# Two state-space layers and two attention layers on one core: the order of scan phases over images, the round of a projection, and the admission limit on TensorE

## The chip, the cores and the metric

The kernel runs on one core of one Trainium2 chip. The metric is device time in microseconds (us) of one execution, lower is better; the time of a version is the median of its runs. The engines are named as in the profile: PE (TensorE matmul; PEld is its weight load), DVE (VectorE), ACT (ScalarE), POOL (GpSimd), SP (SyncE, which issues the DMAs here).

## The reference

The input is four images of 56 x 56 positions with 96 channels (L = 3136 positions). Four layers follow one another.

- Layer 0: layer norm, a projection to u and z (192 channels each), a selective scan of u in four directions (rows forward and back, columns forward and back), a weighted sum of the four, times silu(z), an output projection with shortcut, then a feed-forward block with gelu.
- Layer 1: the same kind of scan with other weights, with a 3 x 3 depthwise convolution and silu ahead of it, a norm and a product with silu(z) behind it, and beside it a branch of depthwise 3 x 3 convolution, relu and pointwise convolution; the two are fused, normed and added to the input.
- Layers 2 and 3: attention without softmax, and a feed-forward block in a small float format.

The scan is what costs most. For each direction, channel d (192) and state n (16), along the 3136 positions:

```
dt = softplus(W_dt @ (W_x @ u)[:rank] + bias)          # per channel and position
h[d, n] = exp(dt[d] * a[d, n]) * h[d, n] + dt[d] * u[d] * B[n]
y[d]    = sum over n of C[n] * h[d, n]   (+ D[d] * u[d])
```

The images are independent of one another; layer 1 of an image needs layer 0 of the same image only.

## The kernel before

**Phases, chunks, rounds.** A phase is the scan of one layer of one image. There are eight, all of layer 0 first (images 0 to 3), then all of layer 1. A phase has four directions (`ORDER`, pairs of orientation and reversal; orientation 1 reads the columns, so that PE, ACT and POOL read and write the tiles with a stride of 56 elements, called vertical below), a direction has seven chunks of 448 positions, and a chunk has eight rounds r = 4e + q: e is the half of the channels (96 each), q a quarter of the states. That makes 8 x 4 x 7 x 8 = 1792 rounds. In a round, 128 partitions hold 4 states x 32 channels, and three groups g hold the 96 channels.

**One round** (function `scans`, L660 to L700). PE spreads B over the partitions by a bf16 matmul into `b` (`spread_b`, L574). DVE multiplies v = du x b (L667), for two or three of the groups; where it does two, POOL makes the third ahead of time (L645). Which rounds DVE does alone is given by `OWN = (3, 4, 6)`, and by `OWN_TAIL = (3, 4)` in layer 1 from image 1 on. ACT makes the decays da = exp(dt x a) in PSUM (L637), DVE runs three scans of 448 steps (L689), POOL multiplies by C into `hc` (L699), and two rounds later PE adds up over the states into `y` (`add_up`, four matmuls at L727). When a new sum starts, at q = 0, so in rounds r = 2 and 6, PE first loads `y` with the sum of the directions so far, or with D x u (L723, fp32, strided if vertical). ACT copies `y` out (L734). Scan state is carried from chunk to chunk by small ACT copies (L693, L652).

**Preparing the next chunks.** While a chunk is scanned, the next one is prepared (`prepare`, `prepare_on_scalar`): its rows are copied out of PSUM in r = 0 (`rows`, L467 and L469), the step sizes are made by matmuls in r = 1 and 3 (`step_size`, L480) with exp and ln on ACT in r = 2 and 3 (L489, L490), multiplied by u on POOL (L496), parked in DRAM and fetched back spread over the partitions. The chunk after that is begun (`prepare_ahead`): its projection `W_x @ u`, two fp32 matmuls (`project_step`, L428), goes out in r = 6 and r = 7. L428 and L480 share one PSUM buffer, `pp`. The first chunk of an image loads U in r = 5.

**Zero matmuls.** `keep_busy` (L706) adds matmuls with zero weights to the open sum (L714): per round `WARM` = 7.3 less the work counted since the last round, where `spend` (L922) counts work at 1.6 per unit of PE. `add_up` adds two more at q = 0.

**Work beside the scans.** Everything else runs in pieces between the half rounds. `beside` lists what starts with which phase: `load` of images 1 to 3 with phase 0, `middle(i)` (end of layer 0, start of layer 1 of image i) with phases 1 to 4, `fuse(i)` (end of layer 1) and `attend(i)` (layers 2 and 3) with phases 5 to 7; what is left runs alone after the last scan (`late`). A part is a generator that stops at each yield with a place (half round C or F, PSUM banks held) and a cost on ACT (a) and PE (p). `overlap` (L892) lets it go on when `room` (L930) finds the backlog plus its cost within `ACT_LIMIT` = 4.0 and `PE_LIMIT` = 5.0; each half round takes `SPARE` = (0.9, 2.4) off the backlog. The scans count their own PE work by constants of 1.3 (L670). Inside the scans the order of instructions on PE, ACT, DVE and POOL is the order in which this program issues them, and each engine works through its list in order.

**Diagonals.** The depthwise convolutions are matmuls with diagonal weights (L876), which POOL builds (`diagonals`, L858): 18 for `middle` once, and 9 for `fuse` once, in the same buffer.

Of the kernel before, what the change touches and what calls it, by code (L numbers as in the profile page):

```python
# [19 lines left out]
NB = 4  # L20
# [5 lines left out]
NE = 2  # L26
NG = 3
NQ = 4
# [3 lines left out]
NCW = L // CW  # L32
# [6 lines left out]
OWN = (3, 4, 6)  # L39
OWN_TAIL = (3, 4)  # L40

SPARE = (0.9, 2.4)
ACT_LIMIT, PE_LIMIT = 4.0, 5.0
BANKS, LATE_BANKS = 2, 4
DEPTH, LATE_DEPTH = 3, 6

# [4 lines left out]
WD = NE * 128 + NE * C + NE + NE * NQ * NG  # L51

EXP_AND_LN = 6

# [108 lines left out]
class Net:  # L165
    def __init__(self, ctx, tc, aps, at, out):
        self.tc, self.nc, self.aps, self.at, self.out = tc, tc.nc, aps, at, out
        pool = lambda name, **kw: ctx.enter_context(tc.tile_pool(name=name, **kw))
        self.const = pool("const", bufs=1)
        self.big = pool("big", bufs=1)  # L170
        self.psum = pool("psum", bufs=1, space=bass.MemoryType.PSUM)
        self.dram = pool("dram", bufs=1, space=bass.MemoryType.DRAM)
        self.nw, self.nwin, self.depth, self.banks, self.ring = NW, NWIN, DEPTH, BANKS, None
        self.setup()
        self.dg = None
        self.kept = (0, 0, 0)
        self.ready = set()
        self.live, self.g = [], {}
        self.backlog, self.paced = [0.0, 0.0], False
        self.work, self.tables = 0.0, False  # L180
        self.U = [self.big.tile([C, L], F32, name=f"U{e}") for e in range(NE)]
        self.Y = [self.big.tile([C, L], F32, name=f"Y{e}") for e in range(NE)]
        self.wp = pool("work", bufs=2)
        self.scan_pool = ExitStack()
        self.sp = self.scan_pool.enter_context(tc.tile_pool(name="scan", bufs=2))
        self.pool = pool
        d = lambda name, *shape: [self.dram.tile(list(shape), F32, name=f"{name}{i}") for i in range(NB)]
        self.xd, self.xrd = d("x", C, L), d("xr", C, L)
        self.ud, self.zd, self.yd, self.md = d("u", DI, L), d("z", DI, L), d("y", DI, L), d("m", DI, L)
# [17 lines left out]
    def par(self, group, name):  # L207
        a, n = self.at[group][name]
        return self.tiles[group][:, a : a + n]
# [350 lines left out]

    def prepare_ahead(self, far, r):

        if far is not None:
            if r == 2:
                self.parameters(far)
            elif r == 5:
                self.inputs(far)
            elif r > 5:
                self.project_step(far, r - 6)

    def spread_b(self, ch, q):

# [16 lines left out]
    def scans(self):  # L589
# [6 lines left out]

        nc, sp = self.nc, self.sp
        chunks = []
        for l in range(2):
            for i in range(NB):  # L600
                for n, (orient, rev) in enumerate(ORDER[l]):
                    for step in range(NCS):
                        ch = Step()
                        ch.l, ch.i, ch.orient, ch.rev, ch.step = l, i, orient, rev, step
                        ch.k = 2 * orient + rev if l == 0 else orient + 2 * rev
                        ch.c = NCS - 1 - step if rev else step
                        ch.n, ch.first = n, n == 0 and step == 0
                        ch.skip = n == 0
                        ch.last = n == 3 and step == NCS - 1
                        for n_ in ("dt", "du", "cb", "dtc", "duc", "dtd", "dud"):  # L610
                            setattr(ch, n_, [])
                        chunks.append(ch)
        first, second = chunks[:2]
        self.parameters(first)
        self.inputs(first)
# [23 lines left out]
        def begin(n):  # L639
            ch, e, q = rounds[n]  # L640
            b = self.spread_b(ch, q)
            v = sp.tile([128, NG, CS + 2], F32, name="v", bufs=3)
            ahead = NQ * e + q not in (OWN_TAIL if ch.l and ch.i else OWN)
            if ahead:
                nc.gpsimd.tensor_tensor(v[:, 2, TOKENS], ch.du[e][:, 2], ch.cb[q][:, 1], ALU.mult)  # L645
            return b, v, ahead
# [13 lines left out]
        for n, (ch, e, q) in enumerate(rounds):  # L660
            r = NQ * e + q
            c = 1 if ch.step else 0
            way = slice(CS + c, 0, -1) if ch.rev else slice(1 - c, CS + 1)
            end = 1 if ch.rev else CS
            b, v, ahead = nxt
            for g in range(2 if ahead else 3):
                nc.vector.tensor_tensor(v[:, g, TOKENS], ch.du[e][:, g], b, ALU.mult)  # L667
            self.prepare(ch, nexts.get(ch), r)
            self.half_round()
            self.spend((0.7, 0, 1.3, 1.3, 0, 0, 0, 0)[r], (0, 1.3, 0, 1.3, 0, 0, 1.3, 1.3)[r] + 1.3 * (r % NQ == 2))  # L670
            yield "F", n, r
            self.prepare_on_scalar(nexts.get(ch), r)
            ended = late.pop(0) if len(late) == 2 else None
            if ended:
                self.keep_busy(ended[2])
            more = n + 1 < len(rounds)
            if more:
                nxt = begin(n + 1)
            if ended:
                self.add_up(*ended)  # L680
            self.prepare_ahead(afters.get(ch), r)
            self.half_round()
            for g in range(NG):
                if g == 1:
                    yield "C", n, r
                if g == 2 and ended and ended[2] == NQ - 1:
                    self.spend(0.6, 0)
                    self.keep_sums(*ended[:3])
                nc.vector.tensor_tensor_scan(  # L689
                    v[:, g, way], da[g][:, way], v[:, g, way], 0.0, ALU.mult, ALU.add  # L690
                )
                if g == 2 and ch.step < NCS - 1:
                    nc.scalar.copy(ch.par.carry[:, e, q].unsqueeze(2), v[:, :, end : end + 1])  # L693
                if more:
                    decay(n + 1, g)
                    if g == 0:
                        carried(n + 1, nxt[1])
            hc = sp.tile([128, NG, CS], F32, name="hc", bufs=3)
            nc.gpsimd.tensor_tensor(hc, v[:, :, TOKENS], ch.cb[q][:, 0].unsqueeze(1).to_broadcast([128, NG, CS]), ALU.mult)  # L699
            late.append((ch, e, q, hc))  # L700
# [30 lines left out]
    def keep_sums(self, ch, e, q):  # L731

        y = self.in_order(self.Y[e], ch.orient, ch.c * CS, CS)
        self.nc.scalar.copy(y, self.y[:C].rearrange("p (a b) -> p a b", b=HS))  # L734
        if ch.n < 3:
            return
        s = slice(ch.c * CS, (ch.c + 1) * CS) if ch.orient == 0 else slice(0, L)
        if ch.orient == 0 or ch.last:
            self.nc.sync.dma_start(self.yd[ch.i][C * e : C * e + C, s], self.Y[e][:, s])
        if e == NE - 1:  # L740
            self.kept = (ch.l, ch.i, ch.step + 1)

# [105 lines left out]
    def diagonals(self, *weights):  # L850

        t = self.wp.tile([128, 9, 192], F32, name="dg", bufs=1)
        out, n = [], 0
        for w in weights:
            p = w.shape[0]
            d = t[:p, :, n : n + p]
            for tap in range(9):
                self.nc.gpsimd.tensor_scalar_mul(d[:, tap], self.ident[:p, :p], w[:, tap : tap + 1])  # L858
                yield "F0"
            out.append(d)  # L860
            n += p
        return out

    def conv(self, diag, win, lo, *parts):

# [94 lines left out]
    def middle(self, i):  # L960
# [45 lines left out]

        yield from self.overlap(part, NCW)

        if self.dg is None:
            self.dg = yield from self.run(self.diagonals(par("c128", "1conv_wa"), par("c128", "1conv_wb")[:64]))  # L1010
        dga, dgb = self.dg

        def convolve(c):
# [24 lines left out]
            nc.sync.dma_start(self.ud[i][128:, s], t)  # L1038

        yield from self.overlap(convolve, NCW, 2)  # L1040
        self.ready.add((1, i))

    def run(self, part):
# [11 lines left out]
    def fuse(self, i):  # L1055

        nc = self.nc
        par = self.par
        if len(self.dg) > 1:
            self.dg = yield from self.run(self.diagonals(par("c96", "1dw_w")))  # L1060
        (dgx,) = self.dg

        def part(c):
# [61 lines left out]
            yield from self.gram(0, i, c, x, s)  # L1125


        yield from self.overlap(part, NCW, ready=lambda c: self.kept >= (1, i, c + 1))

    def attend(self, i):  # L1130

# [141 lines left out]
def tile_net(ctx: ExitStack, tc: tile.TileContext, aps, at, out):  # L1273
# [5 lines left out]
    def alone(lanes):  # L1279
# [4 lines left out]

    alone([net.load(0)])

    beside = [
        [net.load(1), net.load(2), net.load(3)], [net.middle(0)], [net.middle(1)], [net.middle(2)], [net.middle(3)],
        [net.fuse(0), net.attend(0)], [net.fuse(1), net.attend(1)], [net.fuse(2), net.attend(2)],
    ]  # L1290
    rounds = 4 * NCS * NE * NQ
    E = mybir.EngineType
    with tc.manual_schedule(engines={E.PE, E.Activation, E.DVE, E.Pool}):
        net.exp_and_ln()
        lanes = []
        for slot, n, r in net.scans():
            p, u = divmod(n, rounds)
            net.slot, net.paced = slot, True
            if slot == "C" and u == 2 and p < 8:

                assert p > 5 or not lanes
                lanes.append(chain(*beside[p]))
                if p == 7:
                    lanes.insert(0, chain(net.fuse(3), net.attend(3)))
            if n > 1 and p < 8:
# [23 lines left out]
```

## Time and profile before

| | before |
|---|---|
| median of 3 runs | 8809.27 us (8805.61 to 8817.11) |
| the profiled execution's own time | 8833.83 us |
| its span in the profile | 8832.1 us |
| first scan starts, last scan ends | 118 us, 8462 us |
| phases 0 to 3 (layer 0) | 1040, 1033, 1028, 1027 us |
| phases 4 to 7 (layer 1) | 1043, 1067, 1055, 1050 us |
| after the last scan | 370 us |
| zero matmuls (L714) | 6066, busy 1631.0 us |
| mean granted PE clock | 0.90 |

In the profile, a group has the line, the engine, the operation, how many, and its busy time. A matmul with fp32 operands makes two rows. A row of the busy time by stretch has the stretch (us from the span's start), its length, then busy us and instructions of PE, PEld, DVE, ACT and POOL, the granted PE clock, the DMA share and GB/s. A row of the waits has who waited for whom, the total in us, how often, and the longest. Ends of matmuls are modelled, so PE shows as busy somewhat beyond its work.

### The profile page before, as it was taken

The page shows a single profiled execution, that of the slowest core. Times are in us where ns is not written, and L with a number is a line of the kernel's source. Part 1 is how long each engine was busy: PE and PEld are TensorE (multiplying, and loading weights), DVE is VectorE, ACT ScalarE, POOL GpSimd, SP SyncE. Part 2 cuts the span into 40 slices and gives each one's busy share as a digit, 9 for nine tenths or more (in the row PEclk, how much of TensorE's full clock was granted, in tenths as well). Part 3 has the DMA queues.
Part 4 walks back from the last instruction along what each step waited for, and adds up shares of the span by engine and source line. Part 5 has one row for each costly group of instructions (what it writes and reads, how often), then busy time and mean ns, then how long its engine had stood idle before and what let it go on. Part 6 is the DMA issues. An engine that isn't in the chain of part 4 may idle for free.

```text
span 8832.1 us, 122725 instructions
## 1 busy us (share of the span) xinstructions
PE 7589.0 (86%) x34408; PEld 2805.6 (32%) x34408; DVE 7950.4 (90%) x10933; ACT 5910.0 (67%) x12541; POOL 7597.3 (86%) x4075
## 2 busy tenths in 40 slices
PE   6888888797889888898889978988899888998897
PEld 3332223232333223332233323333233332333344
DVE  5999999989998999989998999999999999999941
ACT  5777667676776667766676655667666677666636
POOL 4888999989998999989988899899999999989930
PEclk8888989899998999989898889988899888998986
DMA  5677677677777677766776676667776667666721
GB/s 145 165 175 170 159 186 174 157 167 170 181 163 168 152 182 173 173 160 149 188 171 164 155 175 164 147 152 166 181 168 158 145 162 188 165 157 155 172 73 46
DMA packets 951348, 1418.02 MB, mean 161 GB/s; under 512 B 176578, under 2 KB 943812, under 8 KB 949796
## 3 DMA queue, kind: packets, MB, share of 16 engines
q1 hardware_dynamic: 949888, 1408.37, 67.1%
q8 instruction: 270, 4.42, 0.2%
q14 instruction: 418, 3.42, 0.1%
q10 hardware_dynamic: 772, 1.80, 0.1%
HBM read 1141.42 MB, written 268.14 MB: 160 GB/s over the span
## 4 chain that ended last, share of the span: by engine, by line
PE 43%; DVE 28%; ACT 10%; issue 9%; DMA 5%; POOL 2%; SPq 1%; DVEq 0%; POOLq 0%; ACTq 0%
DVE v L689 20%; PE y L727 8%; DVE v L667 7%; PE y L714 6%; PE y L723 6%; PE pp L428 5%; PE ps L876 4%; ACT da L637 3%; PE b L574 3%; PE pp L480 3%; DMA du<-dd 2%; POOL hc L699 1%; PE ps L779 1%; PE ps L799 1%; DMA cb<-cd 1%
## 5 line engine op out<-in xcount | busy, mean ns | idle before, releaser
L699 POOL TENSOR_TENSOR hc<-v,cb 128x1344 f32<-128x1344 f32 x1792 | 5169.4, 2885 | 662.6 <-DVE v L689 377.6
L689 DVE TENSOR_TENSOR_SCAN v<-da,v 128x449 f32<-128x449 f32 (+1 forms) x5376 | 5521.6, 1072 | 57.9 <-ACT v L652 33.1
L637 ACT ACTIVATE da<-dt,na 128x448 f32<-128x448 f32 x5376 | 3396.5, 634 | 1475.5 <-DVE v L689 1445.0
L667 DVE TENSOR_TENSOR v<-du,b 128x448 f32<-128x448 f32 x4172 | 2332.5, 605 | 247.1 <-PE b L574 181.1
L727 PE MATMUL y<-hc,four 128*32 128x448 f32 x14336 | 1937.3, 616 | 1.8 <-POOL hc L699 1.7
L714 PE MATMUL y<-w,zeros 128*96 128x448 bf16 x6066 | 1631.0, 389 | 0.0
L574 PE MATMUL b<-cf,sel 128*128 128x448 bf16 x1792 | 675.5, 377 | 1025.6 <-DVE v L667 1021.1
L645 POOL TENSOR_TENSOR v<-du,cb 128x448 f32<-128x448 f32 x1204 | 1373.5, 1141 | 97.1 <-DMA cb<-cd 58.2
L714 PEld LDWEIGHTS <-zeros 128*96 128x96 bf16 x6066 | 738.4, 130 | 1364.2 <-issue 1143.6
L428 PE MATMUL pp<-U,wd 96*128 96x448 f32 x896 | 691.6, 860 | 12.3 <-DMA U<-u 12.3
L727 PEld LDWEIGHTS y<-hc,four 128*32 128x32 f32 x14336 | 295.6, 113 | 1157.4 <-issue 727.2
L723 PE MATMUL y<-Y,ident 96*96 96x448 f32 x672 | 546.3, 903 | 37.6 <-ACT Y L734 23.0
L496 POOL TENSOR_TENSOR duc<-dtc,U 96x448 f32<-96x448 f32 x448 | 560.4, 1251 | 4.6 <-ACT dtc L490 4.6
L876 PE MATMUL ps<-win,dg 64*64 64x220 f32 (+9 forms) x1980 | 528.7, 467 | 5.9 <-ACT w L1023 5.0
L693 ACT COPY carry<-v 128x3 f32<-128x3 f32 x1536 | 298.4, 194 | 278.2 <-DVE v L689 277.3
L480 PE MATMUL pp<-cf,wd 12*96 12x448 f32 (+1 forms) x896 | 469.4, 605 | 0.9 <-ACT cf L469 0.8
L489 ACT ACTIVATE dtc<-pp,wd 96x448 f32<-96x448 f32 x448 | 279.2, 623 | 254.3 <-PE pp L480 252.8
L587 POOL TENSOR_TENSOR cf<-cf 64x448 f32<-64x448 f32 x448 | 417.3, 931 | 35.8 <-ACT cf L467 0.8
L734 ACT COPY Y<-y 96x448 f32<-96x448 f32 x448 | 339.3, 757 | 42.6 <-PE y L727 41.6
L876 PEld LDWEIGHTS ps<-win,dg 64*64 64x64 f32 (+2 forms) x1980 | 233.9, 162 | 353.7 <-issue 301.6
L723 PEld LDWEIGHTS y<-Y,ident 96*96 96x96 f32 x672 | 118.6, 187 | 640.9 <-ACT da L637 290.2
L428 PEld LDWEIGHTS pp<-U,wd 96*128 96x128 f32 x896 | 156.8, 219 | 450.1 <-issue 384.8
(423 smaller groups left out, 6050.0 us busy)
## 6 DMA issues: line engine op xcount, KB each, us to landing
cb<-cd SPq DMA_DIRECT2D x3584, 112.0 KB, 4.3
dt<-dd SPq DMA_DIRECT2D x1792, 168.0 KB, 4.4
du<-dd SPq DMA_DIRECT2D x1792, 168.0 KB, 4.2
dd<-dtc SPq DMA_DIRECT2D x448, 168.0 KB, 2.0
dd<-duc SPq DMA_DIRECT2D x448, 168.0 KB, 2.1
U<-u SPq DMA_DIRECT2D x112, 168.0 KB, 4.6
z<-w SPq DMA_DIRECT2D x56, 224.0 KB, 3.0
u<-w SPq DMA_DIRECT2D x56, 224.0 KB, 3.5
```

The costliest lines, as they stand in the source:

```text
L428: self.nc.tensor.matmul(ch.ps.rearrange("p (a b) -> p a b", b=HS), ch.par.wx[:, e], self.in_order(self.U[e], ch.orient, ch.c * CS, CS), st ...
L480: self.nc.tensor.matmul(ps[:C], ch.par.wt[rows, C * e : C * e + C], ch.cf[rows], start=True, stop=True)
L574: self.nc.tensor.matmul(ps, self.sel[:, q], self.upper(ch.cf), start=True, stop=True)
L637: nc.scalar.activation(da[g][:, TOKENS], ch.dt[e][:, g], AF.Exp, scale=ch.par.na[:, e, q, g : g + 1])
L645: nc.gpsimd.tensor_tensor(v[:, 2, TOKENS], ch.du[e][:, 2], ch.cb[q][:, 1], ALU.mult)
L667: nc.vector.tensor_tensor(v[:, g, TOKENS], ch.du[e][:, g], b, ALU.mult)
L689: nc.vector.tensor_tensor_scan(v[:, g, way], da[g][:, way], v[:, g, way], 0.0, ALU.mult, ALU.add)
L699: nc.gpsimd.tensor_tensor(hc, v[:, :, TOKENS], ch.cb[q][:, 0].unsqueeze(1).to_broadcast([128, NG, CS]), ALU.mult)
L714: self.nc.tensor.matmul(self.y[:C], self.zeros, self.some, start=False, stop=False)
L723: nc.tensor.matmul(o, w, self.in_order(a, ch.orient, ch.c * CS, CS), start=True, stop=False)
L727: nc.tensor.matmul(self.y[32 * n : 32 * n + 32], self.four, hc[:, g], start=n == 3, stop=n == 3 or q == NQ - 1,)
L876: self.nc.tensor.matmul(o[:, a - r0 : e - r0, x0:x1], diag[:, tap], win[:, a + dy - lo : e + dy - lo, x0 + dx : x1 + dx], start=n == 0, st ...
```

## The change

1. **Order of phases.** `PHASES = ((0,0), (0,1), (1,0), (0,2), (1,1), (0,3), (1,2), (1,3))`, pairs of layer and image. With phase p starts the work that the phase before it has made possible: `middle(i)` after layer 0 of image i, `fuse(i)` and `attend(i)` after layer 1. So fuse and attend run from phase 3 on; two such parts can be open at a time, and `middle` is put in front.
2. **Projection.** `project_step` goes out in r = 4 and 5, except for the first chunk of an image (r = 6 and 7).
3. **Accounting.** The scans count L723 and the projection's matmuls at 1.5, or 3.0 if vertical, and in the round in which they go out. `PE_LIMIT` is 7.0.
4. **OWN_TAIL** holds from phase 3 on (`LATE_ROUND`), instead of phases 5 to 7.
5. **Diagonals.** They are rebuilt whenever `middle` and `fuse` take turns, and a part waits until nobody uses the other kind.

```diff
+PHASES = ((0, 0), (0, 1), (1, 0), (0, 2), (1, 1), (0, 3), (1, 2), (1, 3))
+
-ACT_LIMIT, PE_LIMIT = 4.0, 5.0
+ACT_LIMIT, PE_LIMIT = 4.0, 7.0
...
+LATE_ROUND = 3 * 4 * NCS * NE * NQ
...
     def prepare_ahead(self, far, r):
-        if far is not None:
-            if r == 2:
-                self.parameters(far)
-            elif r == 5:
-                self.inputs(far)
-            elif r > 5:
-                self.project_step(far, r - 6)
+        if far is None:
+            return
+        if r == 2:
+            self.parameters(far)
+        elif r == 5:
+            self.inputs(far)
+        e = self.projected(far, r)
+        if e in (0, 1):
+            self.project_step(far, e)
+
+    def projected(self, far, r):
+        return r - (6 if far.first else 4)
...
-        for l in range(2):
-            for i in range(NB):
+        for l, i in PHASES:
...
-            ahead = NQ * e + q not in (OWN_TAIL if ch.l and ch.i else OWN)
+            ahead = NQ * e + q not in (OWN_TAIL if n >= LATE_ROUND else OWN)
...
-            self.spend((0.7, 0, 1.3, 1.3, 0, 0, 0, 0)[r], (0, 1.3, 0, 1.3, 0, 0, 1.3, 1.3)[r] + 1.3 * (r % NQ == 2))
+            far = afters.get(ch)
+            strided = [1.5 + 1.5 * ch.orient] * (r % NQ == 2)
+            if far and self.projected(far, r) in (0, 1):
+                strided.append(1.5 + 1.5 * far.orient)
+            self.spend((0.7, 0, 1.3, 1.3, 0, 0, 0, 0)[r], 1.3 * (r in (1, 3)) + sum(strided))
...
+    def diagonal(self, kind, *weights):
+
+        while self.dg_users and self.dg_kind != kind or self.dg_kind == "":
+            yield
+        if self.dg_kind != kind:
+            self.dg_kind = ""
+            self.dg = yield from self.run(self.diagonals(*weights))
+            self.dg_kind = kind
+        self.dg_users += 1
...
-        if self.dg is None:
-            self.dg = yield from self.run(self.diagonals(par("c128", "1conv_wa"), par("c128", "1conv_wb")[:64]))
+        yield from self.diagonal("conv", par("c128", "1conv_wa"), par("c128", "1conv_wb")[:64])
...
-        yield from self.overlap(part, NCW, ready=lambda c: self.kept >= (1, i, c + 1))
+        yield from self.overlap(part, NCW, ready=lambda c: self.kept.get((1, i), 0) > c)
+        self.dg_users -= 1
...
+    beside = [[net.load(1), net.load(2), net.load(3)]]
+    beside += [[net.fuse(i), net.attend(i)] if l else [net.middle(i)] for l, i in PHASES[:-1]]
...
-                assert p > 5 or not lanes
-                lanes.append(chain(*beside[p]))
+                lanes.insert(len(lanes) * PHASES[p - 1][0], chain(*beside[p]))
```

More of the change, by code (lines that the diff above doesn't have):

```diff
@@ L175, in __init__ @@
         self.dg = None
-        self.kept = (0, 0, 0)
+        self.kept = {}
+        self.dg_kind, self.dg_users = None, 0
         self.ready = set()
@@ L598, in scans @@
         chunks = []
-        for l in range(2):
-            for i in range(NB):
[L601 to L612, printed above, removed]
+        for l, i in PHASES:
+            for n, (orient, rev) in enumerate(ORDER[l]):
+                for step in range(NCS):
+                    ch = Step()
+                    ch.l, ch.i, ch.orient, ch.rev, ch.step = l, i, orient, rev, step
+                    ch.k = 2 * orient + rev if l == 0 else orient + 2 * rev
+                    ch.c = NCS - 1 - step if rev else step
+                    ch.n, ch.first = n, n == 0 and step == 0
+                    ch.skip = n == 0
+                    ch.last = n == 3 and step == NCS - 1
+                    for n_ in ("dt", "du", "cb", "dtc", "duc", "dtd", "dud"):
+                        setattr(ch, n_, [])
+                    chunks.append(ch)
         first, second = chunks[:2]
@@ L740, in keep_sums @@
         if e == NE - 1:
-            self.kept = (ch.l, ch.i, ch.step + 1)
+            self.kept[ch.l, ch.i] = ch.step + 1
     def factor(self, *x):
@@ L1058, in fuse @@
         par = self.par
-        if len(self.dg) > 1:
-            self.dg = yield from self.run(self.diagonals(par("c96", "1dw_w")))
+        yield from self.diagonal("dw", par("c96", "1dw_w"))
         (dgx,) = self.dg
@@ L1125, in part @@
             yield from self.gram(0, i, c, x, s)
-        yield from self.overlap(part, NCW, ready=lambda c: self.kept >= (1, i, c + 1))
+        yield from self.overlap(part, NCW, ready=lambda c: self.kept.get((1, i), 0) > c)
+        self.dg_users -= 1
     def attend(self, i):
@@ L1285, in tile_net @@
     alone([net.load(0)])
[L1287 to L1290, printed above, removed]
+    beside = [[net.load(1), net.load(2), net.load(3)]]
+    beside += [[net.fuse(i), net.attend(i)] if l else [net.middle(i)] for l, i in PHASES[:-1]]
     rounds = 4 * NCS * NE * NQ
```

## The prediction

> **What bounds the kernel now.** I read the page first.
>
> ```profile
> span 8832.1 us, 122725 instructions
> PE 7589.0 (86%) x34408; PEld 2805.6 (32%) x34408; DVE 7950.4 (90%) x10933; ACT 5910.0 (67%) x12541; POOL 7597.3 (86%) x4075
> PE 43%; DVE 28%; ACT 10%; issue 9%; DMA 5%; POOL 2%; SPq 1%; DVEq 0%; POOLq 0%; ACTq 0%
> DVE v L689 20%; PE y L727 8%; DVE v L667 7%; PE y L714 6%; PE y L723 6%; PE pp L428 5%; PE ps L876 4%; ACT da L637 3%; PE b L574 3%; PE pp L480 3%; DMA du<-dd 2%; POOL hc L699 1%; PE ps L779 1%; PE ps L799 1%; DMA cb<-cd 1%
> ```
>
> DVE is the fullest engine, yet PE carries more of the chain, so the two take turns. The busy time by stretch, cut at the first scan of each phase, shows how much is left to win. Lines 1 and 3 are phases 3 (layer 0, image 3) and 5 (layer 1, image 1), line 2 is the tail after the last scan.
>
> ```profile
> 3219.39:4246.58 1027.19, 877.24 (x3980) 305.81 (x3980) 970.55 (x1275) 705.56 (x1442) 933.00 (x491) 0.92 0.72 169
> 8461.71:8832.10 370.39, 313.45 (x1386) 187.07 (x1384) 77.60 (x243) 192.88 (x443) 31.09 (x28) 0.76 0.17 47
> 5289.56:6356.26 1066.70, 937.22 (x4315) 345.83 (x4314) 998.08 (x1401) 694.00 (x1565) 969.02 (x531) 0.90 0.69 161
> ```
>
> Over the eight phases the scans take 8343 us and DVE is busy for 7852, so 491 us of DVE idle and 370 us of tail are all there is. DVE's waits inside the scans name the idle time's causes:
>
> ```profile
> DVE v L667 <- PE b L574: 181.1, 179, 3.9
> DVE ps L794 <- ACT rs L792: 80.9, 54, 5.5
> DVE v L689 <- ACT v L652: 33.1, 49, 2.1
> ```
>
> The rest is small: some 75 us in waits on PE by the phase work, 50 on POOL and "issue". To see where b is late I cut one chunk of phase 3 that carries a convolution (37.5 us) into its rounds r=0 to 7:
>
> ```profile
> 3890.72:3895.82 5.10, 5.10 (x28) 1.71 (x28) 4.12 (x7) 3.44 (x7) 3.49 (x3) 1.00 1.08 225
> 3895.82:3900.34 4.52, 4.52 (x18) 1.55 (x18) 4.12 (x7) 3.92 (x8) 4.36 (x4) 1.00 0.84 196
> ...
> 3913.62:3918.17 4.55, 2.85 (x23) 1.10 (x22) 4.55 (x8) 4.51 (x7) 3.94 (x2) 1.00 0.93 227
> 3918.17:3922.18 4.01, 3.58 (x9) 0.77 (x12) 4.01 (x7) 3.29 (x8) 3.44 (x3) 0.73 1.09 236
> 3922.18:3928.24 6.06, 6.06 (x34) 1.86 (x27) 4.11 (x6) 2.12 (x5) 6.03 (x4) 0.90 1.08 269
> ```
>
> In r=5 PE has 2.85 us to do and DVE is full; in r=7 and r=0 PE is solid and DVE loses 2 and 1 us. A chunk without phase work (4036.75 to 4071.18) takes 34.4 us with 33.9 of DVE: nothing to win there. Averaged over layer 1, vertical chunks, the time from scan to scan is 5.75 us after r=7 and 5.32 after r=0, 4.3 to 5.1 elsewhere.
>
> **Projection moved (r=6, 7 to r=4, 5).** The chain through that chunk gives PE's price of each step: two vertical L428 rows 1.82 us, L723 1.65, four L727 0.89, L480 0.92, one L714 0.20, b 0.2 to 0.3, six convolution rows 2.4. In horizontal chunks the timeline has the next start 0.75 us after L723's. L428 stands in r=6 beside L723 today and r=4, 5 have little. I added these prices up along the instruction order of both kernels, from one b matmul to the next. Vertical layer 1 chunks go from 3.1, 2.6, 6.5, 5.0 (r=4 to 7) to 4.0, 4.3, 5.5, 3.5. PE can run about 3 us (one round's scans) ahead of DVE, so what hurts is pairs of rounds: their sum over 10.5 us (two DVE rounds of 4.25 plus 2) totals 215 us before, 102 after. The 181 us of waits for b should fall in that proportion at best; since a convolution chunk's five heaviest rounds (r=4 to r=0) stay near 26 us (25.7 before, 26.6 after), I keep 55%: **-80 us**. The phase work's own waits (about 155 us) queue behind the same PE work: -30 (0 to -60). The moved step waits on more: `pp` has one buffer, and the L489 read of the second step size in r=3 must finish before L428 starts in r=4. ACT does that in r=3's second half (623 ns), and what would queue behind a late L428 is b of the round after; half of that in each of 224 chunks, 70 us, bounds it; PE's spare time in r=3 hides it, I take 0. The first chunk of an image keeps r=6, and SP's queue is untouched: 9450 SP instructions in both orders.
>
> **Zero matmuls.** Because the strided matmuls are now counted at 1.5 or 3.0, 951 of 6066 L714 go: 951 x 0.20 = 190 us of PE. L714 is 6.6% of the chain inside the scans, 550 us for 6066, so at most 86 us of path; that is part of the pair sums above and is not counted again. Against it stands the clock. Consecutive 3.41 us stretches of the quiet chunk:
>
> ```profile
> 4056.53:4059.94 3.41, 1.75 (x12) 0.41 (x11) 3.41 (x5) 1.75 (x5) 3.41 (x3) 1.00 0.92 217
> 4059.94:4063.35 3.41, 0.52 (x2) 0.32 (x2) 3.41 (x6) 2.14 (x5) 3.39 (x2) 1.00 1.02 239
> 4063.35:4066.76 3.41, 3.41 (x12) 0.56 (x10) 3.41 (x6) 2.12 (x5) 2.84 (x3) 0.50 1.03 229
> ```
>
> A stretch with 0.52 us of PE is followed by one at half clock; one with 1.75 isn't. Over all such stretches of the trace (each matmul's end taken 0.16 us earlier, for the pipeline) every one under 35% busy was followed by half clock, about two thirds at 35 to 45%, and 4 of 1263 above 75%. The Trainium skill, "TensorE: Matmul & The Clock Gate", section "Why this matters for your kernels", asks only for no idle gap over about 3 us. By that rule the removed zeros are free, since no round loses all its work, and the whole 86 us could come (8563 on top of my sum); by the rows the limit lies near 40% busy, and thinner rounds can halve the clock. In the after order r=3 of vertical chunks falls to 1.8 or 1.9 us (from 2.7 to 2.9) while r=5 rises from 2.3-2.6 to 3.7-4.3. So I expect the half-clock stretch to move from r=6 to r=4. There it meets vertical L428, whose start to start is 0.82 us at full clock and 0.91 at half: nearly free. By the rows the sum is then my 8649, and 8880 if it lands elsewhere (the slow rival). I take 0, from -40 to +233, because the row with the stretch is nearest.
>
> **The limit 5 to 7** lets longer pieces start in a loaded round; its effect is in the pair sums.
>
> **Order of phases.** The fuse convolutions (PE work of 15 us a chunk) met vertical chunks in phases 5 to 7 (PE sums 32 to 36 us). In new phases 3 and 5 they fall into horizontal chunks at 31 to 34. Chunks of the first kind lost about 3 us over DVE, of the second about 2; some 20 chunks: **-20** (0 to -40).
>
> **DVE to POOL.** OWN_TAIL now covers five phases: 56 L667 fewer on DVE (0.57 us each, from pairs of 1.15) is -32; POOL gains 56 x 1.14 = 64 us. Three ffn pieces move from the tail into the scans, +6. In phases 4 and 6 only `middle` runs, and my sums give DVE 957 us and POOL 968, so there POOL is the floor, 11 us each; part of it lies in idle time that DVE has anyway, so of 22 I take +16. Net **-10**. The diagonals are built six times, not twice: 54 more L858 at 0.55 us, 30 us on POOL. Queued behind them are hc and then y; in the trace all 27 together kept another engine waiting for 0.7 us. Cover: POOL has 80 to 95 us idle in 1000; without it, +30. I take 0. The new wait in `diagonal` holds only the phase work: by the order, the last convolution for phase 6 goes out in the fourth direction of phase 4, a whole phase early.
>
> **Tail.** 18 ffn pieces instead of 21 remain after the last scan (ACT 399 instructions, was 445; PE 883, was 962), but image 3's own chain, fuse, attention, seven pieces, attention, seven pieces, is unchanged. Scaling 370 by 10% gives -37, the unchanged chain gives 0: **-20**.
>
> **Sum.** -80 -30 -20 -10 -20 = -160 us on a span of 8832.1 (execution 8833.83), which stands 25 us above the median of 8809.27. The same 160 off the median is 8649: **8650 us**, own range 8580 to 8720.
>
> **Rivals.**
> - All waits on PE vanish and the chunks come near the quiet one: -181 -80 on waits and -50 from the other terms, some -310: 8500. For it: quiet chunks lose 0.5 us. Against: convolution chunks still need 34.5 us of PE, with r=1 and r=3 thin and the rest crowded.
> - The overloads stay, since 25.7 us became 26.6 in the five heavy rounds of such a chunk: only -20 -10 -20 remains: 8760.
> - POOL becomes the bound. Its highest share of a phase is 91.6% (967.14 of 1055.34). If it can't be filled further, five phases of 968 us take 1057 each, 5285 against 5242 now, +43; three phases gain 30, the tail 20: 8800. Against: the quiet chunk has POOL at 95% (32.81 of 34.43).
> - Slower: the clock. If the thin r=3 adds one half-clock stretch per chunk where PE's work isn't strided, it costs 1.7 us of PE, and in the 137 chunks whose PE work is over 27 us by my sums it is on the path: 137 x 1.7 = 233 - 160, about 8880. It decides once the share of half clock in the scans, 18.5% now, passes some 25%.
>
> **Chances.** Forecast 0.52, overloads stay 0.17, waits vanish 0.15, POOL 0.09, clock 0.07. Within 0.2% (17.6 us, about what a measurement of this kernel can tell from no change) lies most of the POOL case. Faster 0.87, same 0.06, slower 0.07. From 8520 to 8790 leaves out half of the "vanish" case, half of POOL and the clock.
>
> **What would show it.** Right: waits of L667 for b near 100 us; time after r=7 near 4.7 us and r=0 under 5; half clock moved from r=6 to r=4; DVE busy near 7826 us in the scans; tail near 350. Wrong: b's waits unchanged (limit 7 crowds the same rounds), POOL over 95% busy in phases 4 and 6 with DVE waiting for v L645 or duc, or the mean clock in the scans under 0.88.

## The result and the profile after

| | before | after |
|---|---|---|
| median | 8813.19 us (4 runs) | 8691.61 us (4 runs, 8679.16 to 8701.20) |
| ratio, 95% interval | 1 | 0.986 (0.9842 to 0.9878) |
| span of the profiled execution | 8832.1 us | 8699.2 us |
| scans, first to last | 8343 us | 8215 us |
| DVE busy in the scans, and idle | 7853, 491 us | 7823, 393 us |
| after the last scan | 370 us | 363 us |
| half clock in the scans | 18.5% | 21.5% |

The change makes the kernel 1.4% faster. Forecast were 8650 us and a range of 8580 to 8720, and 8692 lies inside. The page's first lines after:

```profile
span 8699.2 us, 120910 instructions
PE 7537.3 (87%) x33457; PEld 2729.5 (31%) x33457; DVE 7914.4 (91%) x10877; ACT 5917.0 (68%) x12541; POOL 7675.3 (88%) x4185
```

Busy time by stretch, phases 3 (layer 0 of image 2, beside fuse of image 0), 4 (layer 1 of image 1, beside middle of image 2) and the tail:

```profile
3175.60:4217.63 1042.03, 923.33 (x4246) 337.03 (x4244) 998.66 (x1410) 711.63 (x1597) 971.06 (x533) 0.90 0.70 165
4217.63:5226.79 1009.16, 869.99 (x3870) 293.27 (x3870) 956.78 (x1249) 716.42 (x1464) 968.72 (x537) 0.90 0.73 173
8336.53:8699.24 362.71, 313.74 (x1292) 192.23 (x1291) 71.92 (x223) 173.71 (x397) 27.97 (x25) 0.71 0.16 44
```

DVE's and POOL's busy time in phase 4, 957 and 969 us, is what was worked out (957 and 968), but the phase takes 1009. DVE's waits in the scans, some of the rows, first before (those that the prediction doesn't show), then after:

```profile
DVE v L689 <- POOL v L645: 21.3, 20, 4.6
DVE v L667 <- POOL duc L496: 20.4, 20, 1.6
...
DVE v L667 <- DMA du<-dd: 8.5, 3, 3.5
```

```profile
DVE ps L808 <- ACT rs L806: 74.2, 63, 6.0
DVE v L677 <- PE b L585: 54.0, 53, 5.4
DVE v L703 <- POOL v L655: 50.6, 70, 2.0
DVE v L677 <- DMA du<-dd: 48.9, 6, 16.1
...
DVE v L677 <- POOL duc L501: 38.2, 34, 1.6
```

The wait for b fell from 181 to 54 us, more than forecast. New in its place are more waits on POOL (v from 21 to 51 us, duc from 20 to 38) and on DMA. Of the six DMA waits the longest, 16.1 us, ends just before the first scan; before, the same wait of 16.1 us ended at 117 us, ahead of the stretch from 118 us that the rows count. Inside the scans it is 33 us in five waits, against 8.5 in three. Three of the five, 8.2 to 9.2 us each, come up again below. The rounds of a convolution chunk, now in phase 2 (a vertical one like that of the prediction, but of layer 1):

```profile
2754.52:2759.07 4.55, 4.55 (x26) 1.94 (x23) 4.12 (x6) 3.11 (x7) 4.52 (x3) 1.00 1.07 260
...
2776.70:2781.25 4.55, 4.55 (x19) 1.16 (x19) 4.55 (x8) 4.51 (x7) 4.11 (x2) 1.00 1.00 232
2781.25:2785.26 4.01, 4.01 (x25) 1.31 (x21) 4.01 (x6) 3.29 (x8) 3.45 (x3) 1.00 1.11 228
2785.26:2789.27 4.01, 4.01 (x35) 1.83 (x33) 4.01 (x6) 2.32 (x6) 3.84 (x3) 1.00 0.97 221
```

Round 5 is filled, rounds 6 and 7 take DVE's own 4.01 us, and the clock is full in all eight rounds; the chunk takes 34.75 us, where that of the prediction took 37.52. So the aim was met where it was aimed. The losses stand elsewhere: six chunks with the start of a convolution take over 42 us, three of fuse (46.0 to 49.2 us, phases 3, 5 and 7) and three of middle (44.4 to 44.7, phases 1, 4 and 6). The kernel before has two such chunks, in phases 1 and 5.

### The profile page after: what moved, and what is told of

It reads as the page before. It is cut to its first block, busy times and chain, and to the rows that moved or that the text cites. A ratio compares the mean times of both kernels' runs of the same rounds, so it can differ in the third digit from the quotient of the medians.

```text
span 8699.2 us, 120910 instructions
## 1 busy us (share of the span) xinstructions
PE 7537.3 (87%) x33457; PEld 2729.5 (31%) x33457; DVE 7914.4 (91%) x10877; ACT 5917.0 (68%) x12541; POOL 7675.3 (88%) x4185
## 5 line engine op out<-in xcount | busy, mean ns | idle before, releaser
L677 DVE TENSOR_TENSOR v<-du,b 128x448 f32<-128x448 f32 x4116 | 2300.3, 605 | 168.6 <-PE b L585 54.0
L741 PE MATMUL y<-hc,four 128*32 128x448 f32 x14336 | 1972.0, 626 | 9.2 <-POOL hc L713 8.6
L655 POOL TENSOR_TENSOR v<-du,cb 128x448 f32<-128x448 f32 x1260 | 1435.6, 1139 | 106.2 <-DMA cb<-cd 63.8
L728 PE MATMUL y<-w,zeros 128*96 128x448 bf16 x5115 | 1466.8, 404 | 0.0
L728 PEld LDWEIGHTS <-zeros 128*96 128x96 bf16 x5115 | 633.8, 135 | 1324.2 <-issue 1175.1
L433 PE MATMUL pp<-U,wd 96*128 96x448 f32 x896 | 672.3, 837 | 13.7 <-DMA U<-u 13.7
L900 PE MATMUL ps<-win,dg 64*64 64x220 f32 (+8 forms) x1962 | 517.8, 459 | 4.5 <-DMA win<-m 4.5
L485 PE MATMUL pp<-cf,wd 6*96 6x448 f32 (+1 forms) x896 | 501.6, 642 | 3.7 <-ACT cf L474 2.5
L585 PEld LDWEIGHTS <-sel 128*128 128x128 bf16 x1792 | 186.3, 104 | 345.2 <-issue 280.8
```

The costliest lines, as they stand in the source:

```text
L433: self.nc.tensor.matmul(ch.ps.rearrange("p (a b) -> p a b", b=HS), ch.par.wx[:, e], self.in_order(self.U[e], ch.orient, ch.c * CS, CS), st ...
L585: self.nc.tensor.matmul(ps, self.sel[:, q], self.upper(ch.cf), start=True, stop=True)
L728: self.nc.tensor.matmul(self.y[:C], self.zeros, self.some, start=False, stop=False)
L741: nc.tensor.matmul(self.y[32 * n : 32 * n + 32], self.four, hc[:, g], start=n == 3, stop=n == 3 or q == NQ - 1,)
L900: self.nc.tensor.matmul(o[:, a - r0 : e - r0, x0:x1], diag[:, tap], win[:, a + dy - lo : e + dy - lo, x0 + dx : x1 + dx], start=n == 0, st ...
```

## Experiments

**Theory first held:** the early projection unwinds PE's crowding in r=6 and 7, and that is the gain. Rivals: the fewer zero matmuls; the order of phases.

**e1: the kernel before with the early projection alone.**

```diff
-            elif r > 5:
-                self.project_step(far, r - 6)
+        e = r - (6 if far.first else 4)
+        if e in (0, 1):
+            self.project_step(far, e)
...
-(0, 1.3, 0, 1.3, 0, 0, 1.3, 1.3)[r] + 1.3 * (r % NQ == 2)
+(0, 1.3, 0, 1.3, 1.3, 1.3, 0, 0)[r] + 1.3 * (r % NQ == 2)
```

> The kernel before with one part of the change: the projection in r=4 and 5 (first chunk of an image in r=6 and 7), its old count of 1.3 moved with it; old order of phases, limit 5, old OWN_TAIL. My theory, that the crowding of PE in r=6 and 7 was what made b late: DVE's waits of v L667 for b fall from 181 us to 60-100 us and the time from 8813 to 8720-8750. Rival, that the fewer zero matmuls (the new counts) did it: waits for b stay above 140 us and the time above 8780. Rival, that the order of phases did it: the same, above 8780.

Measured: 8636.26 us, ratio 0.979 (0.9774 to 0.9805). That is more than the whole change gains, and more than I expected. Its waits for b:

```profile
DVE v L669 <- PE b L576: 32.4, 24, 5.9
```

DVE's idle time in the scans is 308 us, against 491 before and 393 after the whole change. The very chunk that the prediction cut into rounds takes 34.0 us here, was 37.5. So the early projection carries the gain, and the rest of the change loses. One thing e1 doesn't keep apart: with the count moved, it also has 5630 zero matmuls instead of 6066. The pair e3 and e10 below speaks to that.

**e5: the changed kernel with the projection back in r=6 and 7** (`return r - 6`).

> The changed kernel with the projection back in r=6 and 7, counted there at 1.5 and 3.0; all else as changed. My theory: the waits for b come back, from 54 us to 120-170 us, and the time rises from 8692 to 8750-8790. Rival, fewer zero matmuls did it: waits for b stay under 90 us, the time within 20 us of 8692. Rival, the order of phases: the same.

Measured: 8779.20 us, 0.9952 (0.9939 to 0.9965). The time comes back as expected (88 us over the changed kernel), the waits for b only to 92 us, under the 120 expected; waits for v L655 rise from 51 to 72. So part of the loss shows at other waits than b's; which way it gets there was not followed.

**e4 and e3: the old counts of 1.3, or the old limit of 5.0, in the changed kernel.**

```diff
-            strided = [1.5 + 1.5 * ch.orient] * (r % NQ == 2)
+            strided = [1.3] * (r % NQ == 2)
...
-                strided.append(1.5 + 1.5 * far.orient)
+                strided.append(1.3)
```

> The changed kernel with the strided matmuls counted at 1.3 again (in the rounds where they now are), so that zero matmuls come back and longer pieces are let in sooner; all else as changed. My theory: the counts matter little, the time stays within 25 us of 8692 and the waits for b under 90 us, while the share of half clock in the scans falls from 21.5% toward 19%. Rival, fewer zero matmuls did it: 8740-8780 and waits for b over 110 us. Third, that the lower clock is a loss: faster than 8692 by 20 us or more.

> The changed kernel with the limit on TensorE's backlog at 5.0 instead of 7.0; all else as changed. My theory: nearly nothing, within 20 us of 8692, since pair sums of PE's work are set by the projection. Rival, that longer pieces let the phase work end earlier and so shorten the tail: tail over 375 us instead of 363, time 8700-8730. Rival, that limit 7 crowds rounds: faster, waits for b under 40 us.

Measured: e4 8744.13 us, 0.9914 (0.9899 to 0.9929), waits for b 72 us, half clock 21.9%. My number for e4 was wrong by 27 us or more, and half clock did not fall. The time lies in the range of the rival (fewer zeros did it), the waits for b do not. e3 8699.32 us, 0.9865 (0.9849 to 0.9882): no difference, though tail and scans shift (382 and 8188 us).

**e10: both old together**, since limit 7 with low counts lets in more than limit 5 did.

> The changed kernel with the old counts of 1.3 and the old limit of 5.0 together; the interleaved order, the early projection and the wide OWN_TAIL stay. Theory that new counts and limit 7 only balance each other, so that the whole change is the projection's gain less the order's cost: 8675 to 8710, the changed kernel's 8692. Rival, that the new counts are worth their 52 us by themselves, whatever the limit: 8735 or more.

Measured: 8670.68 us, 0.9844 (0.9822 to 0.9866), 4 us under the theory's range and, by the ratios, not to be told from the changed kernel. With the old counts, limit 7 costs 73 us (8671 to 8744); with the new ones it costs nothing (8699 to 8692). So the new counts win back what the wider limit gives away. The zero matmuls don't decide: at the same limit of 5, e10 has 5577 and e3 5156, and e10, with more, is not the slower one (8671 and 8699 us). The counts also govern when phase work is let in, so no run changes the zeros alone.

**e2: the changed kernel in the old order of phases**, OWN_TAIL from phase 5 as before.

```diff
-PHASES = ((0, 0), (0, 1), (1, 0), (0, 2), (1, 1), (0, 3), (1, 2), (1, 3))
+PHASES = ((0, 0), (0, 1), (0, 2), (0, 3), (1, 0), (1, 1), (1, 2), (1, 3))
...
-LATE_ROUND = 3 * 4 * NCS * NE * NQ
+LATE_ROUND = 5 * 4 * NCS * NE * NQ
```

> The changed kernel with the old order of phases (layer 0 of all images, then layer 1) and OWN_TAIL from phase 5 as before; projection, counts, limit 7 and the diagonals' bookkeeping as changed. New theory, that the interleaved order with the wider OWN_TAIL is a loss: about 8590-8640, that is faster than the changed kernel's 8692 by 50 us or more. Rival, that order is worth something and the loss against the projection alone (8636) lies in counts or limit: 8680-8740.

Measured: 8648.31 us, 0.9801 (0.9781 to 0.9820), level with e1. So interleaving with the wider OWN_TAIL costs some 43 us here (52 by the ratios to the kernel before), where -20 and -10 were forecast.

**e6: OWN_TAIL in phases 3, 5 and 7 only.**

```diff
-(OWN_TAIL if n >= LATE_ROUND else OWN)
+(OWN_TAIL if n // (LATE_ROUND // 3) in (3, 5, 7) else OWN)
```

> The changed kernel with OWN_TAIL only in phases 3, 5 and 7, where fuse and attend run, so in as many chunks as before; all else as changed. Theory that POOL, with one more multiplication in phases 4 and 6, is their floor: DVE's waits for v L655 fall from 51 us to about 30, phases 4 and 6 go from 1009 and 1020 to about 995 and 1005, the time to 8655-8680. Rival, DVE's 32 us are a gain as I forecast: 8692 to 8715.

Measured: 8683.68 us, 0.9844 (0.9825 to 0.9864). Neither side: the waits for v L655 fall to 43 us only, phases 4 and 6 take 1014 us each instead of the 995 and 1005 expected, and the time can't be told from 8692. Moving 56 multiplications between DVE and POOL made no difference that these runs can show.

**Where the order costs.** SP's queue in the changed kernel, in the long chunk of phase 1 (start, length, engine, line, operation, tiles):

```profile
1726.22 0.36 SPq L518 DMA_DIRECT2D du<-dd  x1
1740.25 0.47 SPq L911 DMA_DIRECT2D win<-m  x1
1740.77 1.52 SPq L518 DMA_DIRECT2D du<-dd  x3
1742.34 5.64 SPq L526 DMA_DIRECT2D cb<-cd  x12
```

Nothing is issued for 13.7 us. The waits of SP have that row:

```profile
SPq L911 <- PE y L728: 13.8, 1, 13.8
```

The window load is the fourth into three buffers and waits until PE is through the first window's nine taps. Behind it stand the next chunk's du and twelve cb; DVE then waits 9.2 us for du. Phases 4 and 6 have the same (8.2 and 8.5 us). Long waits for a window are not new. The largest rows of SP's waits for window loads, before and after:

```profile
SPq L887 <- PE b L574: 111.1, 19, 12.7
```

```profile
SPq L911 <- PE y L728: 38.6, 3, 13.8
```

All window loads together made SP wait 166 us before and 102 after. New is that three of these waits hold a du back until DVE has to wait for it. In e1 and e2, with the old order, that happens once, in phase 1 (DVE waits 7.8 and 7.9 us there, the chunk takes 43.4 and 43.3). So two of the three belong to the order. The three stand where the diagonals of middle have just been built; in phase 2, where they are still there, no such chunk is long.

**e8: the second window fetched when the part's first convolution begins.**

```diff
-            wb, _ = self.window(self.md[i][128:], 64, c)
             yield "C0"
             yield "C1 p3.8"
+            wb, _ = self.window(self.md[i][128:], 64, c)
```

> The changed kernel with the second window of convolve fetched when its first convolution begins, not together with the first window; nothing else. Theory that the fourth window, which waits on SP's queue 13.8 us for PE to release the first and holds the next chunk's du and cb behind it, makes the three chunks of 44.4 to 44.7 us in phases 1, 4 and 6: these fall to about 36 us, DVE's waits for DMA from 49 to under 20 us, the time by 15 to 40 us. Rival, that these chunks are long because PE is crowded: no change within 15 us, the long chunks stay over 42.

Measured: 8663.25 us, 0.9814 (0.9795 to 0.9834). The chunk of phase 1, in the changed kernel and in e8:

```profile
1702.16:1746.82 44.66, 33.27 (x129) 10.89 (x128) 34.01 (x45) 24.73 (x51) 33.97 (x20) 0.86 0.47 111
```

```profile
1699.75:1735.08 35.33, 30.37 (x125) 9.91 (x124) 33.91 (x44) 21.07 (x48) 34.98 (x21) 0.90 0.68 162
```

DVE does the same 34 us of work in both; 9 us of waiting are gone. Those of phases 4 and 6 go to 36.0 us too. Inside the scans, DVE's waits for du fall from 33 us to 5.

**e9: the diagonals built on ACT instead of POOL.**

```diff
-                self.nc.gpsimd.tensor_scalar_mul(d[:, tap], self.ident[:p, :p], w[:, tap : tap + 1])
+                self.nc.scalar.activation(d[:, tap], self.ident[:p, :p], AF.Copy, scale=w[:, tap : tap + 1])
```

> The changed kernel with the diagonals built on ACT instead of POOL; all else as changed. My prediction took the four extra builds at nothing, bounded by 30 us of POOL. Theory that they cost: 15 to 35 us faster than 8692, the first chunks of phases 3, 5 and 7 shorter. Rival, hidden: within 15 us.

Measured: 8664.37 us, 0.9816 (0.9798 to 0.9833). The gain lies in the chunks in which the diagonals are built: 37.5 to 33.6 us in phase 1; 36.3 and 38.0 to 34.5 and 33.2 in phase 4; 36.4 to 34.5 in phase 3. DVE's waits for v L655 fall from 51 to 21 us.

**e11: fuse's loads of y issued before its first convolution.** At the start of fuse in phase 3, PE itself waits for a load:

```profile
PEld ps L1108 <- DMA w<-y: 3.5, 1, 3.5
```

```diff
+            ya, yb = self.get(d[:128], 128, s), self.get(d[128:], 64, s)
             ps = self.ps()[:C, :CW]
             yield from self.conv(dgx, win, lo, (ps, c * CR, CR))
-            ya, yb = self.get(d[:128], 128, s), self.get(d[128:], 64, s)
```

> The changed kernel with fuse's loads of y issued before its first convolution, not after it; all else as changed. Theory that PE, waiting 3.5 us for the first y in phases 3, 5 and 7, falls to half clock and makes the chunks of 46 to 49 us: these fall under 42, the time by 10 to 30 us. Rival, that these chunks are long because three parts start at once whatever the loads do: no change within 10 us.

Measured: 8658.31 us, 0.9826 (0.9806 to 0.9845). The chunk of phase 3, changed kernel and e11:

```profile
3245.92:3293.05 47.13, 44.46 (x159) 14.74 (x158) 35.74 (x50) 22.84 (x54) 36.03 (x21) 0.82 0.70 167
```

```profile
3251.65:3289.55 37.90, 37.01 (x160) 13.59 (x159) 35.48 (x50) 22.91 (x54) 35.99 (x21) 1.00 0.93 213
```

Almost the same instructions take 9.2 us less, and the clock is full instead of 0.82. In the changed kernel half clock follows on PE's wait, from 3263 to 3277 us, and three rounds there take 8.8, 9.0 and 7.5 us, against 6.0, 4.5 and 5.5 in e11. With the loads issued early both the wait and the half clock are gone, so the 9.2 us belong to the two together; the wait alone is 3.5 us.

**e12: the three edits together; e13: the three on the old order.**

> The changed kernel with the late second window, the diagonals on ACT and the early loads of y together. If the costs of the new order are separate, the gains of 28 and 27 us add, with the y loads some 8620-8640; if they are one and the same wait seen from three sides, 8655-8670.

> The same three edits on the old order of phases with OWN_TAIL from phase 5 (8648 without them). If the new order's cost is the more frequent restart of phase work, the edits are worth little here: 8630-8650, and the interleaved version with the edits comes level with it. If the order costs something else, this one is faster by 20 us or more than the interleaved one with the edits.

Measured: e12 8590.08 us, 0.9757 (0.9733 to 0.9781); e13 8615.44 us, 0.9776 (0.9755 to 0.9797). e12 is faster than even the 8620 to 8640 expected. The gains add within what the runs can tell (28 + 27 + 33 = 88 and 102 by the medians, 41 + 39 + 30 = 110 and 91 by the ratios), so these are three separate costs. In e12 none of the six chunks takes over 38 us, and DVE's waits there, some of the rows (the wait of 16.1 us ahead of the first scan falls outside the stretch here):

```profile
DVE v L677 <- PE b L585: 38.8, 49, 4.7
...
DVE v L703 <- POOL v L655: 18.3, 23, 1.6
...
DVE v L677 <- DMA du<-dd: 2.8, 1, 2.8
```

The trace of e12 is of its longest execution, 8622 us; the other three took 8588 to 8592. With the three edits the two orders are level: the intervals overlap. e12 has the lowest median, 2.4% under the kernel before. The old order gains only 33 us from the edits, and its traces (e2, e13) show where: in phase 1, with its one start and one build of middle (1015 to 998 us), and in phase 5, with the one start and build of fuse (1038 to 1021). The other phases change by 6 us or less; the tail is 17 us shorter there, which was not followed.

## Why the prediction was right, and where it was off

The total came within 42 us in part by luck: the gain of the projection was forecast 77 us too small, and a loss from the order of phases and its builds, some 45 us, stood in the sum as a gain of 20. The mechanism of the main term was right.

- **Projection: right in mechanism, too small.** Forecast -110 with the waits it frees; alone it gives -187 (e1), and taking it out of the change costs 88 (e5). I kept 55% of the waits for b, and took 47% (102 of 215) for the best that could be reached; 30% stayed in the change, 18% in e1. So the pair sums point the right way but are no bound, and that is the mis-sized term: -80 forecast for b, -149 measured in e1. Why the sums show too little was not tested. One candidate is the clock, which they leave out: in the chunks shown it went from 0.73 in r=6 and 0.90 in r=7 to 1.00. Of the signs named, in vertical chunks of layer 1, the time after r=0 fell from 5.32 to 4.33 us (under 5 was asked), that after r=7 from 5.75 to 4.99 (near 4.7 was asked).
- **Zero matmuls and clock: no loss from them showed, as forecast.** Half clock rose from 18.5 to 21.5% of the scans, and more zeros at the same limit were not slower (e3, e10). It left r=6, as forecast, but settled in r=2 and r=3, not in r=4: in vertical chunks of layer 1 it fell from 2.3 to 1.05 us in r=6 and rose from 1.26 to 2.5 in r=2 and from 0.75 to 1.6 in r=3. The limit "near 40%" is also softer than the prediction says: in a like count over the trace of before, 85 of 471 stretches between 45 and 75% busy were followed by half clock too. The rival with the clock fell: 21.5% is short of the 25% named. The thin round ahead of the half clock is r=1, as in these two rounds, r=1 and r=2, of a vertical chunk of phase 1:

```profile
2033.00:2037.01 4.01, 1.25 (x9) 0.25 (x9) 4.01 (x6) 2.67 (x6) 3.85 (x3) 1.00 0.36 75
2037.01:2041.56 4.55, 4.42 (x14) 0.97 (x14) 4.55 (x8) 3.29 (x8) 4.39 (x4) 0.62 0.15 41
```

- **Limit: right that it needs no term of its own**, but only because the new counts stand against it (e4, e10).
- **Order of phases: wrong in sign.** Forecast -20 for horizontal chunks under fuse's convolutions; e2 says some +43 together with OWN_TAIL. The failed step is what a start of phase work costs, for which the prediction has no term. In the old order one chunk in phase 1 and one in phase 5 pay for it; interleaved, fuse starts anew in phases 3, 5 and 7 and middle in 1, 4 and 6, each after a build. A start cost 8 to 11 us (e8, e11). Estimated from the chunks that became shorter, the two extra starts of middle are 17 us (e8), the two of fuse 17 (e11), the four extra builds 18 (e9), together 52, beside the 43 to 52 measured. The -20 itself is neither shown nor excluded: with the three edits the interleaved order is 25 us ahead by the medians, 17 by the ratios, with overlapping intervals (e12, e13).
- **Diagonals: the step "I take 0" failed.** The bound of 30 us without cover was nearer: building them on ACT gives 27 us by the medians, 39 by the ratios (e9; that takes the two builds of before along, and a build takes ACT 0.36 us a tap instead of 0.52). POOL's 80 to 95 us of idle in 1000 were no cover: DVE needs a v from POOL in five or six rounds of eight, and its waits for v fell by 30 us once the builds were gone. The trace of before named 0.7 us as what waited for the builds directly; the delay shows up at the next instructions of the queue instead.
- **SP "untouched": wrong.** The number of issues is the same (9448 in both traces), what stands behind a waiting one is not (e8). Equal counts on a queue say nothing about that.
- **DVE to POOL: -10 forecast, none measured (e6).** A sign that was named for being wrong did appear: POOL is busy for 96.0 and 95.1% of phases 4 and 6 (968.72 of 1009.16, 969.88 of 1020.28 us), and DVE waits more for v and duc. But with less work on POOL there (e6) these phases were no faster, so POOL was not what held them.
- **Tail: -20 forecast, -8 measured.** Over the runs the tail lies between 343 and 382 us, so the 8 mean little, and what sets it was not tested.

Terms by the runs: projection -187, order with its starts, builds and OWN_TAIL about +45, counts and limit some 0 to +20, against -122 in all. The last term is within the runs' spread, and that of the order is known to some 10 to 15 us.

## What to carry to other kernels

Between two engines that take turns, sum each engine's work over pairs of neighbouring rounds, not over the whole loop: moving two matmuls by two rounds gained more than the whole change did. When work is reordered, price every start: first loads, the first full buffer, builds on a busy queue; list for each issuing queue which instruction can block it and what stands behind it. Try the parts of a mixed change alone, since here one part carried it and others took 65 us back.

## What the hardware showed beyond expectation

- A DMA issue that waits on an in-order queue costs twice: 13.8 us of waiting, then 7.2 us to issue the fifteen that stood behind (du and cb above, about 0.5 us each).
- The share of half clock says little about the time: 18.9% of the scans at 8636 us (e1), 20.8% at 8648 (e2), 21.5% at 8692 (the change) and at 8590 (e12). Where it falls says more: one load that kept PE waiting for 3.5 us at the start of fuse, with the half clock that followed, cost 9 us.
- A row of the fp32 matmul that loads `y` (L723) takes, from start to start in the trace of before, 0.82 us if vertical (stride of 224 bytes) at full clock and 0.83 at half; if contiguous, 0.38 and 0.75. So the strided row hardly feels the clock. For L428 vertical it is 0.86 and 0.91 to 0.96, where the prediction has 0.82 and 0.91.
